# Later filter taps, eps as a bias, a last block by column halves and wider gathers in a Mamba block with a top-1 expert layer

## The chip, the cores and the metric

The kernel runs on one core of a Trainium2 chip. The metric is the device time of one execution in microseconds (us), as the median of several runs. The core's engines are written as in the profile: PE (TensorE, with its weight loads as PEld), DVE (VectorE), ACT (ScalarE), POOL (GpSimd) and SP (SyncE). They run side by side, each through its own queue in order, and wait for each other by semaphores.

## The reference

Two residual layers, each followed by a normalisation over 256 features, on 4096 tokens in one sequence:

```python
xz = input_tensor @ W_in                      # 256 -> 1024
conv_in, gated = xz[..., :512], xz[..., 512:]
convolved = silu(causal_conv(conv_in, 4 taps, per channel) + conv_b)
x_dbl = convolved @ W_x                       # 1 + 16 + 16 columns
delta = softplus(x_dbl[..., :1]);  Bm, Cm = x_dbl[..., 1:17], x_dbl[..., 17:]
deltaA  = exp(delta * A);  deltaBx = delta * Bm * convolved[..., :16]
h = deltaA * h + deltaBx;  y = sum(h * Cm)    # token after token
attn = ((y + convolved * D_param) * silu(gated)) @ W_out
x = layernorm(x + attn)
e = argmax(x @ Wr.T + br)                     # one of 8 experts
x = layernorm(x + relu(x @ W1[e].T + b1[e]) @ W2[e].T + b2[e])
```

The hidden width of an expert is 1024. layernorm is (x − mean) / sqrt(variance + 1e-05).

## The kernel before

**Two phases that overlap.** The tokens go through the Mamba block in 8 chunks of 512 (`TB`, `NB`). After that they are sorted by expert: 32 blocks of 128 rows (`SURE`), each of one expert, are gathered from the DRAM tensor `x1d`, put through the expert, and scattered to the output. The main loop runs over `k`, one chunk at a time, and works on several chunks at once: the in-projection of chunk k, the middle of chunk a = k−1, the end of chunk b = k−2, and the sorting of chunk c = k−3. The order of PE's instructions is that of the source (`manual_schedule` for PE); for the other engines a scheduler orders the instructions as it expects them to become ready, so an instruction's place in the source is only one of the things that set its place in a queue.

**One chunk.** `project(k, c)` makes 128 channels for c = 0 to 7. PE multiplies (`pm`, L722). For c < 4 they are the convolution's channels: ACT copies them to `xc` (L729) and makes the last tap with the bias into `acc` (L731), and DVE adds the other three taps (L735, three instructions over 128 by 512). Two projections later ACT makes their silu, `cv` (L742). For c of 4 and more ACT makes the silu of the gate, `sg` (L727). Between the projections stand the other chunks' steps:

- `gauge(a)` and `gauge_out(a)`: `x_dbl` of chunk a. PE multiplies and transposes (`px` L757, `pxo` L770), ACT copies, DVE adds two halves to `xd` (L780), and softplus follows as a chain of small instructions over 128 by 4: `e` (L785), its Exp on ACT (L786, for which ACT loads another table of functions), `s`, `w`, `q` on DVE (L792 to L801), and then `sr` (L804, L807), which holds delta, delta·B and C.
- `scan(a)`: PE transposes `sr` to `pt` (L816), ACT makes exp(delta·A), DVE runs the recurrence and multiplies with C to `hC` (L830).
- `gate(b)`: PE spreads `hC` as `py` (L842), DVE makes `cv` (L849), POOL and DVE the product `sg` (L854).
- `project_out(b, j)` for 128 tokens each: PE makes `po` (L890), DVE adds it to the input in `xb` (L894) and takes statistics (L898, L899). After the fourth, DVE adds eps (L904), ACT takes the root (L905), DVE makes `nma` (L908), ACT writes the normalised rows `x1` (L911), and SP stores them to `x1d`.
- `rank(c)`: the place of each token within its expert, as `row` (L971) and `col`; POOL makes the table `rowh` from `row` (L979), in four instructions, and for the last three chunks DVE does. `place(c)` (PE, L990) and a table with lookups turn them into the lists of row numbers, `tidx`, and of weights, `widx`.

**One expert block.** `prefetch` issues the indirect transfers on POOL: the block's rows `xg` (L500) and its expert's weights `we` (L517), two blocks ahead (`AHEAD`). `turn` transposes the rows (`pg`, L546), `hidden` multiplies with the first matrix (`ph`, L574) and ACT (L583, half 0) and DVE (L585, half 1) write relu into `hT`. `close` multiplies with the second matrix in 8 matmuls of 256 columns into `pe` (L599), DVE makes `xs`, the rows with the bias of the expert (L617). `finish` adds them to `r` (L624) and calls `layernorm` (L253 to L260): statistics and their aggregate on DVE, eps added on DVE (L257), root on ACT (L258), reciprocal and `y` on DVE. `scatter` writes `y` to its tokens by an indirect transfer on POOL (L637). At block 31, the last (`SURE - 1`), nothing is left to lie beside this chain.

**Longer blocks.** The blocks 17, 20, 23, 26 and 29 (`LONG`) take 32, 32, 32, 64 and 64 further rows (`ROOM`; `MORE` is its largest entry, 64), which a second gather brings (L500, named `long` in the profile) and a second layernorm and scatter finish. Tokens that find no room anywhere would go through blocks beyond the 32 under a condition.

**What the change touches.** `layernorm`, the list `further` in the lookup, `prefetch`, `close`, `scatter`, `project` with L735, L904 in `project_out`, and the main loop between `gauge_out(a)` and `project_out(b, 0)`.

Of the kernel before, what the change touches and what calls it, by code (L numbers as in the profile page):

```python
# [37 lines left out]
F32 = mybir.dt.float32  # L38
# [3 lines left out]
AF = mybir.ActivationFunctionType  # L42
ALU = mybir.AluOpType
# [4 lines left out]
P = 128  # L48
T, D = 4096, 256
DI, NS, KC = 512, 16, 4  # L50
NE, FF = 8, 1024
TB = 512
# [4 lines left out]
CC = DI // P  # L57
FC = FF // P
# [5 lines left out]
SURE = 32  # L64
# [10 lines left out]
ROOM = (32, 32, 32, 64, 64)  # L75
EXTRA, LESS, MORE = len(ROOM), min(ROOM), max(ROOM)
# [5 lines left out]
EPS = 1e-5  # L82
# [6 lines left out]
OC = OB + FC  # L89
# [10 lines left out]
def mamba_moe(  # L100
# [82 lines left out]
    def load_later():  # L183
# [6 lines left out]
        nc.sync.dma_start(brb, br.to_broadcast([P, NE]))  # L190
        nc.sync.dma_start(x1d[T : T + 1, :], lists[0:1, 0:D])

    ident = const.tile([P, P], F32, name="ident")
    make_identity(nc, ident)
    ones = const.tile([P, P], F32, name="ones")
# [50 lines left out]
        allow_small_or_imprecise_dtypes=True,  # L246
    )

    def layernorm(pool, rows, done, name):

        n = rows.shape[0]
        st = pool.tile([P, 6], F32, tag="st", name=f"st{name}")[0:n, :]
        nc.vector.bn_stats(st, rows)  # L253
        mv = pool.tile([P, 2], F32, tag="mv", name=f"mv{name}")[0:n, :]
        nc.vector.bn_aggr(mv, st)
        sd = pool.tile([P, 1], F32, tag="sd", name=f"sd{name}")[0:n, :]
        nc.vector.tensor_scalar(sd, mv[:, 1:2], EPS, None, ALU.add)  # L257
        nc.scalar.activation(sd, sd, AF.Sqrt)  # L258
        nc.vector.reciprocal(sd, sd)
        nc.vector.tensor_scalar(done, rows, mv[:, 0:1], sd, ALU.subtract, ALU.mult)  # L260

# [18 lines left out]
    def table(b0, nb, columns, rows, early):  # L280
# [155 lines left out]
        def lookup():  # L436

            pi = bank("tr", f"pi{b0}", 2)
            n = nb + longer
            for h in range(LH):  # L440
                nc.tensor.matmul(
                    pi[:, 0:n], lhsT=lists[:, h * P : (h + 1) * P], rhs=pick[:, h, :],
                    start=(h == 0), stop=(h == LH - 1),
                )
            codes = small("codes", [n])
            nc.scalar.copy(codes, pi[:, 0:n])
            half = small("half", [n])
            nc.vector.tensor_scalar(half, codes, 0.0, -float(T + 1), ALU.is_gt, ALU.mult)
            tidx = const.tile([P, n], I32, name=f"tidx{b0}")
            nc.vector.scalar_tensor_tensor(tidx, codes, float(T), half, ALU.add, ALU.add)  # L450
            for b in range(nb):
                index[b0 + b] = rows, tidx[:, order(b0, b)]
            for b, x in LONG.items() if longer else ():
                further[b] = tidx[0 : ROOM[x], nb + x : nb + x + 1]

        return lookup

# [35 lines left out]
    xgs, wes, turned, hid, last, open_, ys = {}, {}, {}, {}, {}, {}, {}  # L493


    xgf, openf, yf, ends_, wide_, xss, seldom_in = {}, {}, {}, {}, {}, {}, []
    current = 0

    def gather(to, rows, at):
        nc.gpsimd.indirect_dma_start(  # L500
            out=to, out_offset=None, in_=x1d[0:rows, :],
            in_offset=bass.IndirectOffsetOnAxis(ap=at, axis=0),
        )

    def prefetch(b):
        for n in range(b, min(b + AHEAD, SURE - 1) + 1):
            if n in index and n not in xgs:
                xgs[n] = m3.tile([P, D], F32, tag="xg", name=f"xg{n}", bufs=4)
                gather(xgs[n], *index[n])
                if n in LONG:  # L510
                    ends_[n] = a2.tile([P, CC, KC - 1 + TB], F32, tag="xc", name=f"long{n}")
                    ends_[n] = ends_[n].rearrange("p c t -> p (c t)")
                    xgf[n] = ends_[n][0 : more_of(n), 0:D]
                    gather(xgf[n], index[n][0], further[n])
            if n in weights and n not in wes:
                wes[n] = held_weights[n % SLOTS]
                nc.gpsimd.indirect_dma_start(  # L517
                    out=wes[n][:, :], out_offset=None, in_=experts,
                    in_offset=bass.IndirectOffsetOnAxis(ap=weights[n], axis=0),
                    bounds_check=NE * P - 1, oob_is_err=False,  # L520
                )

    def more_of(b):
        return ROOM[LONG[b]] if b in LONG else 0
# [64 lines left out]
    def close(b, half):  # L589
        we, hT = wes[b], hid[b]  # L590
        if half == 0:
            open_[b] = bank("o", f"pe{b}")
        py = open_[b]

        def out_weights(fc):
            return we[:, O2 + fc * D : O2 + (fc + 1) * D]

        for fc in range(half * FC // 2, (half + 1) * FC // 2):
            nc.tensor.matmul(  # L599
                py[:, 0:D], lhsT=hT[:, fc, 0:P], rhs=out_weights(fc),  # L600
                start=(fc == 0), stop=(fc == FC - 1),
            )
        if half == 0:
            return
        if b in LONG:

            openf[b], n = bank("o", f"pf{b}"), more_of(b)
            for fc in range(FC):
                g = fc * n % P
                nc.tensor.matmul(  # L610
                    openf[b][g : g + n, 0:D], lhsT=hT[:, fc, P:], rhs=out_weights(fc),
                    start=(fc < P // n), stop=(fc >= FC - P // n), tile_position=(0, g),
                )
        xss[b] = m2.tile([P, D], F32, tag="xs", name=f"xs{b}")

        with tc.issue_after(last[b].ins):
            nc.vector.tensor_tensor(xss[b], xgs[b], we[:, OC : OC + D], ALU.add)  # L617
        if b != SELDOM:
            finish(b)

# [12 lines left out]
            layernorm(m2, r, yf[b], f"f{b}")  # L633

    def scatter(b):
        for rows, at in ((ys[b], index[b][1]), *(((yf[b], further[b]),) if b in LONG else ())):
            moved = nc.gpsimd.indirect_dma_start(  # L637
                out=out, out_offset=bass.IndirectOffsetOnAxis(ap=at, axis=0),
                in_=rows, in_offset=None, bounds_check=T - 1, oob_is_err=False,
            )  # L640

            tc.declare_no_dep(moved.ins, group="rows", reason="blocks have no row in common")
            tc.add_to_no_dep_group("rows", moved.ins)
# [60 lines left out]

    def project(i, c):

        s = st[i]
        xTb = s["xTb"]  # L710
        if c == 0:
            if i == 0:
                s["xc"] = a2.tile([P, CC, KC - 1 + TB], F32, tag="xc", name="xc0")
                nc.gpsimd.memset(s["xc"][:, :, 0 : KC - 1], 0.0)
            s["cv"] = a3.tile([P, CC, TB], F32, tag="cv", name=f"cv{i}")
            s["sg"] = a3.tile([P, CC, TB], F32, tag="sg", name=f"sg{i}")
        xc, cv, sg = s["xc"], s["cv"], s["sg"]
        pm = bank("mm", f"pm{i}_{c}")

        for at in (slice(0, first), slice(first, TB)) if i == c == 0 else (slice(0, TB),):  # L720
            for dc in range(DC):
                nc.tensor.matmul(  # L722
                    pm[:, at], lhsT=win[:, dc, c * P : (c + 1) * P], rhs=xTb[:, dc, at],
                    start=(dc == 0), stop=(dc == DC - 1),
                )
        if c >= CC:
            evicted = nc.scalar.activation(sg[:, c - CC, :], pm, AF.Silu)  # L727
        else:
            nc.scalar.copy(xc[:, c, KC - 1 :], pm)  # L729
            acc = a3.tile([P, TB], F32, tag="acc", name=f"acc{i}_{c}")  # L730
            evicted = nc.scalar.activation(  # L731
                acc, pm, AF.Identity, scale=cw[:, c, KC - 1 : KC], bias=cb[:, c : c + 1]
            )
            for k in range(KC - 1):
                nc.vector.scalar_tensor_tensor(  # L735
                    acc, xc[:, c, k : k + TB], cw[:, c, k : k + 1], acc, ALU.mult, ALU.add
                )
            s["acc", c] = acc
        if ("acc", c - 2) in s:

            with tc.issue_after(evicted.ins):
                nc.scalar.activation(cv[:, c - 2, :], s["acc", c - 2], AF.Silu)  # L742
        if c == CC and i + 1 < NB:

            after = st[i + 1]["xc"] = a2.tile(
                [P, CC, KC - 1 + TB], F32, tag="xc", name=f"xc{i + 1}"
            )
            nc.gpsimd.tensor_copy(after[:, :, 0 : KC - 1], xc[:, :, TB : TB + KC - 1])
# [137 lines left out]
    def project_out(i, j):  # L886
# [14 lines left out]
            return  # L901
        mv = s_["mv"]
        sd = s_["sd"] = a2.tile([P, JT], F32, tag="sda", name=f"sda{i}")
        nc.vector.tensor_scalar(sd, mv[:, :, 1], EPS, None, ALU.add)  # L904
        nc.scalar.activation(sd, sd, AF.Sqrt)  # L905
        nc.vector.reciprocal(sd, sd)
        nm = a2.tile([P, JT], F32, tag="nma", name=f"nma{i}")
        nc.vector.scalar_tensor_tensor(nm, mv[:, :, 0], -1.0, sd, ALU.mult, ALU.mult)  # L908
# [103 lines left out]
    def have(i):  # L1012
        return 0 <= i < NB
# [4 lines left out]
    for k in range(NB):  # L1018
# [26 lines left out]
        project(k, 3)  # L1045
        if have(a):
            gauge_out(a)
        if have(b):
            project_out(b, 0)
        expert(fill[3])  # L1050
# [125 lines left out]
```

## Time and profile before

| what | value |
|---|---|
| median of 3 runs | 490.08 us (489.82 to 491.45) |
| the profiled execution | 486.77 us |
| its span | 485.0 us |
| mean granted PE clock | 0.996 |
| PE busy | 471.0 us (97%) |
| DVE busy | 346.9 us (72%) |
| ACT busy | 218.8 us (45%) |
| POOL busy | 186.9 us (39%) |
| DMA | 89.55 MB, mean 185 GB/s |

The span is that of the recorded instructions, in us from the first; the execution's own time is 1.8 us longer. In the views below, a group line gives the instructions' count, their busy time, the mean in ns, and the idle time of the engine before them with its releaser. A timeline line gives start, duration, engine, source line and operation, output and inputs with shapes, how many instructions are drawn together, and in brackets the idle time before with what ended it. A window's line gives the window and its length, then the busy time of PE, PEld, DVE, ACT and POOL with counts, the PE clock, the share of the DMA engines' time, and GB/s. A line of the view of waits gives the engine and instruction that waited, what it waited for, the total in us, the number of times and the longest.

### The profile page before, as it was taken

To read this page: it belongs to the slowest core of one execution; us is meant where nothing else is said; L and a number is where in the kernel's file an instruction comes from. 1 tells how busy PE (TensorE), PEld (TensorE's weight loads), DVE (VectorE), ACT (ScalarE), POOL (GpSimd) and SP (SyncE) were. 2 spreads that over 40 slices of the span, in tenths; PEclk is the share of its full clock that TensorE was granted. 3 is DMA by queue.
4 is the path that set the end of the run, shared out by engine and by line. 5 is a ranking of instruction groups with operands and counts; after the bars stand their busy time and mean duration, and the time that the engine had idled before them with its cause. 6 is when DMAs were issued, how large, how long until landed. Compare 5 with 4: busy or idle time off the path is not lost.

```text
span 485.0 us, 7589 instructions
## 1 busy us (share of the span) xinstructions
PE 471.0 (97%) x2602; PEld 351.9 (73%) x2602; DVE 346.9 (72%) x1160; ACT 218.8 (45%) x452; POOL 186.9 (39%) x193
## 2 busy tenths in 40 slices
PE   8999999999999999999999999999999999999993
PEld 5444555545454676776989999999989898989882
DVE  2577969797999997986989879554465656555362
ACT  3777678887778776655633122122121212112120
POOL 2001203444427454342524332444344456635531
PEclk9999999999999999999999999999999999999998
DMA  7401012030316926423577857999985289868800
GB/s 236 152 10 45 0 45 86 14 118 0 95 39 243 393 91 234 146 110 112 204 249 270 309 177 311 352 327 368 357 276 205 49 340 294 256 223 297 311 18 22
DMA packets 23049, 89.55 MB, mean 185 GB/s; under 512 B 4898, under 2 KB 14629, under 8 KB 19298
## 3 DMA queue, kind: packets, MB, share of 16 engines
q0 software_dynamic: 8672, 74.29, 42.4%
q1 hardware_dynamic: 13378, 14.50, 9.3%
q8 instruction: 21, 0.34, 0.3%
q10 hardware_dynamic: 960, 0.27, 0.3%
q14 instruction: 18, 0.15, 0.1%
HBM read 87.35 MB, written 9.54 MB: 200 GB/s over the span
## 4 chain that ended last, share of the span: by engine, by line
PE 73%; DVE 14%; issue 6%; DMA 3%; ACT 2%; POOL 1%; POOLq 0%; SPq 0%; ACTq 0%
PE ph L574 24%; PE pe L599 22%; PE pm L722 12%; PE po L890 8%; DVE acc L735 5%; DVE cv L849 2%; PE pg L546 2%; PE px L757 2%; DMA xg<-x1d,tidx 1%; DMA win<-in_W_in 1%; PE py L842 1%; PE pf L610 1%; PE pz L990 1%; DVE nma L908 1%; PE pt L816 1%
## 5 line engine op out<-in xcount | busy, mean ns | idle before, releaser
L722 PE MATMUL pm<-xTb,win 128*128 128x512 f32 (+1 forms) x260 | 121.3, 598 | 0.7 <-DMA win<-in_W_in 0.5
L574 PEld LDWEIGHTS ph<-xgT,we 128*128 128x128 f32 x864 | 100.7, 192 | 6.0 <-DVE stm L253 1.2
L574 PE MATMUL ph<-xgT,we 128*128 128x128 f32 x864 | 103.2, 276 | 0.0
L599 PE MATMUL pe<-we,hT 128*128 128x256 f32 x432 | 99.4, 381 | 0.0
L599 PEld LDWEIGHTS pe<-we,hT 128*128 128x128 f32 x432 | 79.7, 190 | 10.2 <-DVE lg L931 0.3
L735 DVE SCALAR_TENSOR_TENSOR acc<-xc,cw,acc 128x512 f32<-128x512 f32 x96 | 71.2, 771 | 16.5 <-ACT acc L731 16.1
L722 PEld LDWEIGHTS pm<-xTb,win 128*128 128x128 f32 x260 | 47.6, 192 | 47.5 <-issue 40.7
L517 POOL DMA_INDIRECT we<-in_experts,widx x32 | 33.9, 1058 | 89.2 <-DVE r L624 28.3
L258 ACT ACTIVATE sdm<-sdm 128x1 f32<-128x1 f32 x32 | 6.5, 202 | 131.0 <-DVE sdm L257 131.0
L890 PE MATMUL po<-wout,sg 128*128 128x264 f32 x256 | 64.1, 392 | 0.0
L854 POOL TENSOR_TENSOR sg<-cv,sg 128x512 f32<-128x512 f32 x22 | 33.9, 1544 | 59.2 <-DVE cv L849 44.1
L890 PEld LDWEIGHTS po<-wout,sg 128*128 128x128 f32 x256 | 46.0, 190 | 10.2 <-issue 2.9
L637 POOL DMA_INDIRECT out<-y,tidx x32 | 32.9, 1027 | 43.1 <-DVE y L260 26.8
L624 DVE TENSOR_TENSOR r<-pe,xs 128x256 f32<-128x256 f32 x32 | 13.5, 422 | 45.4 <-PE pe L599 45.2
L585 DVE TENSOR_SCALAR hT<-ph,we 128x128 f32<-128x128 f32 x108 | 31.5, 342 | 18.7 <-PE ph L574 18.4
L500 POOL DMA_INDIRECT xg<-x1d,tidx x32 | 32.0, 998 | 30.3 <-DVE tidx L450 5.7
L583 ACT ACTIVATE hT<-ph,we 128x128 f32<-128x128 f32 x108 | 31.0, 367 | 25.9 <-PE ph L574 23.3
L979 POOL TENSOR_SCALAR rowh<-lrow,row,code 128x256 f16<-128x256 bf16 x20 | 25.8, 1298 | 26.7 <-DVE row L971 26.7
L849 DVE SCALAR_TENSOR_TENSOR cv<-cv,dp,py 128x256 f32<-128x256 f32 x64 | 28.8, 469 | 2.4 <-PE py L842 2.4
L727 ACT ACTIVATE sg<-pm 128x512 f32<-128x512 f32 x32 | 19.1, 596 | 17.1 <-PE pm L722 14.8
L729 ACT COPY xc<-pm 128x512 f32<-128x512 f32 x32 | 18.6, 581 | 17.0 <-PE pm L722 16.9
L731 ACT ACTIVATE acc<-pm,cb,cw 128x512 f32<-128x512 f32 x32 | 25.1, 784 | 0.0
(221 smaller groups left out, 616.5 us busy)
## 6 DMA issues: line engine op xcount, KB each, us to landing
xb<-in_x SPq DMA_DIRECT2D x8, 512.0 KB, 4.8
x1d<-x SPq DMA_DIRECT2D x8, 512.0 KB, 4.8
xTb<-in_xT SPq DMA_DIRECT2D x7, 512.0 KB, 3.7
win<-in_W_in SPq DMA_DIRECT2D x1, 512.0 KB, 6.2
we<-in_W_outT SPq DMA_DIRECT2D x1, 512.0 KB, 4.8
wout<-in_W_out SPq DMA_DIRECT2D x1, 512.0 KB, 5.7
we<-in_experts,widx POOLq DMA_INDIRECT x32, 10.2
xg<-x1d,tidx POOLq DMA_INDIRECT x32, 6.2
```

The lines of the kernel that those rows point to most:

```text
L500: nc.gpsimd.indirect_dma_start(out=to, out_offset=None, in_=x1d[0:rows, :], in_offset=bass.IndirectOffsetOnAxis(ap=at, axis=0),)
L517: nc.gpsimd.indirect_dma_start(out=wes[n][:, :], out_offset=None, in_=experts, in_offset=bass.IndirectOffsetOnAxis(ap=weights[n], axis=0), ...
L574: nc.tensor.matmul(ph[:, n * w : (n + 1) * w], lhsT=we[:, at : at + P], rhs=xgT[:, dc * w : (dc + 1) * w], start=(dc == 0), stop=(dc == DC ...
L583: nc.scalar.activation(hT[:, fc, :], ph[:, n * w : (n + 1) * w], AF.Relu, bias=bias)
L585: last[b] = nc.vector.tensor_scalar(hT[:, fc, :], ph[:, n * w : (n + 1) * w], bias, 0.0, ALU.add, ALU.max)
L599: nc.tensor.matmul(py[:, 0:D], lhsT=hT[:, fc, 0:P], rhs=out_weights(fc), start=(fc == 0), stop=(fc == FC - 1),)
L637: moved = nc.gpsimd.indirect_dma_start(out=out, out_offset=bass.IndirectOffsetOnAxis(ap=at, axis=0), in_=rows, in_offset=None, bounds_chec ...
L722: nc.tensor.matmul(pm[:, at], lhsT=win[:, dc, c * P : (c + 1) * P], rhs=xTb[:, dc, at], start=(dc == 0), stop=(dc == DC - 1),)
L735: nc.vector.scalar_tensor_tensor(acc, xc[:, c, k : k + TB], cw[:, c, k : k + 1], acc, ALU.mult, ALU.add)
L849: nc.vector.scalar_tensor_tensor(cv[:, c, at], cv[:, c, at], dp[:, c : c + 1], py[:, 0 : TB // 2], ALU.mult, ALU.add,)
L854: eng.tensor_tensor(sg[:, c, :], cv[:, c, :], sg[:, c, :], ALU.mult)
L890: nc.tensor.matmul(po[:, 0 : D + NE], lhsT=sg[:, c, j * P : (j + 1) * P], rhs=wout[:, c, :], start=(c == 0), stop=(c == CC - 1),)
```

## The change

Four edits are made.

1. `eps` is a tile of 128 by 1, filled once on POOL. In `layernorm` and in `project_out` the addition of eps on DVE is gone (L257, L904), and ACT's root reads the variance itself with `eps` as its bias.
2. `project(k, 3)` no longer issues its three taps. A new function `taps` does, and for the fourth group of channels the main loop calls it after `gauge_out(a)`.
3. The last block's second product is made by column halves. `close` is called twice for a block, as before; for block 31 each call now does all 8 matmuls on 128 columns, where it did 4 on 256. The first call makes `xs`, and each adds its half to `r` and takes that half's statistics; the second runs the rest of layernorm over both.
4. The gather of further rows always takes 64 rows (`MORE`). The transposes, products and the scatter use as many as before (`more_of`).

```diff
+    eps = const.tile([P, 1], F32, name="eps")
+    nc.gpsimd.memset(eps, EPS)
...
-    def layernorm(pool, rows, done, name):
+    def layernorm(pool, rows, done, name, st=None):
         n = rows.shape[0]
-        st = pool.tile([P, 6], F32, tag="st", name=f"st{name}")[0:n, :]
-        nc.vector.bn_stats(st, rows)
+        if st is None:
+            st = pool.tile([P, 6], F32, tag="st", name=f"st{name}")[0:n, :]
+            nc.vector.bn_stats(st, rows)
         mv = pool.tile([P, 2], F32, tag="mv", name=f"mv{name}")[0:n, :]
         nc.vector.bn_aggr(mv, st)
         sd = pool.tile([P, 1], F32, tag="sd", name=f"sd{name}")[0:n, :]
-        nc.vector.tensor_scalar(sd, mv[:, 1:2], EPS, None, ALU.add)
-        nc.scalar.activation(sd, sd, AF.Sqrt)
+        nc.scalar.activation(sd, mv[:, 1:2], AF.Sqrt, bias=eps[0:n, :])
...
-                further[b] = tidx[0 : ROOM[x], nb + x : nb + x + 1]
+                further[b] = tidx[0:MORE, nb + x : nb + x + 1]
...
+                    gather(ends_[n][0:MORE, 0:D], index[n][0], further[n])
                     xgf[n] = ends_[n][0 : more_of(n), 0:D]
-                    gather(xgf[n], index[n][0], further[n])
...
+        def add_rows():
+            xss[b] = m2.tile([P, D], F32, tag="xs", name=f"xs{b}")
+            with tc.issue_after(last[b].ins):
+                nc.vector.tensor_tensor(xss[b], xgs[b], we[:, OC : OC + D], ALU.add)
+        if b == SURE - 1:
+            at = slice(half * D // 2, (half + 1) * D // 2)
+            for fc in range(FC):
+                nc.tensor.matmul(
+                    py[:, at], lhsT=hT[:, fc, :], rhs=out_weights(fc)[:, at],
+                    start=(fc == 0), stop=(fc == FC - 1),
+                )
+            if half == 0:
+                add_rows()
+                halves.append(m2.tile([P, D], F32, tag="r", name=f"r{b}"))
+                halves.append(a2.tile([P, 2, 6], F32, tag="sta", name=f"st{b}"))
+            r, sts = halves
+            nc.vector.tensor_tensor(r[:, at], py[:, at], xss[b][:, at], ALU.add)
+            nc.vector.bn_stats(sts[:, half, :], r[:, at])
+            if half == 1:
+                ys[b] = m2.tile([P, D], F32, tag="y", name=f"y{b}")
+                layernorm(m2, r, ys[b], f"m{b}", sts)
+            return
...
-        xss[b] = m2.tile([P, D], F32, tag="xs", name=f"xs{b}")
-        with tc.issue_after(last[b].ins):
-            nc.vector.tensor_tensor(xss[b], xgs[b], we[:, OC : OC + D], ALU.add)
+        add_rows()
...
-        for rows, at in ((ys[b], index[b][1]), *(((yf[b], further[b]),) if b in LONG else ())):
+        for rows, at in ((ys[b], index[b][1]), *(((yf[b], further[b][0 : more_of(b), :]),) if b in LONG else ())):
...
+    def taps(i, c):
+        acc, xc = st[i]["acc", c], st[i]["xc"]
+        for k in range(KC - 1):
+            nc.vector.scalar_tensor_tensor(
+                acc, xc[:, c, k : k + TB], cw[:, c, k : k + 1], acc, ALU.mult, ALU.add
+            )
...
-            for k in range(KC - 1):
-                nc.vector.scalar_tensor_tensor(
-                    acc, xc[:, c, k : k + TB], cw[:, c, k : k + 1], acc, ALU.mult, ALU.add
-                )
             s["acc", c] = acc
+            if c < CC - 1:
+                taps(i, c)
...
-        nc.vector.tensor_scalar(sd, mv[:, :, 1], EPS, None, ALU.add)
-        nc.scalar.activation(sd, sd, AF.Sqrt)
+        nc.scalar.activation(sd, mv[:, :, 1], AF.Sqrt, bias=eps)
...
         project(k, 3)
         if have(a):
             gauge_out(a)
+
+        taps(k, CC - 1)
         if have(b):
             project_out(b, 0)
```

More of the change, by code (lines that the diff above doesn't have):

```diff
@@ L493, in mamba_moe @@
     xgs, wes, turned, hid, last, open_, ys = {}, {}, {}, {}, {}, {}, {}
-    xgf, openf, yf, ends_, wide_, xss, seldom_in = {}, {}, {}, {}, {}, {}, []
+    xgf, openf, yf, ends_, wide_, xss, seldom_in, halves = {}, {}, {}, {}, {}, {}, [], []
     current = 0
```

## The prediction

> **What bounds the kernel.** First the table of windows: busy time of each engine by stretch, PE first.
>
> ```profile
> 100.00:140.00 40.00, 39.26 (x156) 21.02 (x156) 37.02 (x101) 31.93 (x54) 14.61 (x12) 1.00 0.21 66
> 140.00:180.00 40.00, 39.27 (x185) 23.68 (x184) 37.24 (x134) 30.48 (x52) 24.02 (x19) 1.00 0.57 221
> ...
> 260.00:420.00 160.00, 160.00 (x1108) 146.49 (x1107) 102.78 (x396) 31.15 (x112) 74.24 (x74) 1.00 0.78 280
> ...
> 475.00:485.00 10.00, 2.13 (x10) 1.52 (x8) 1.93 (x7) 0.20 (x1) 0.99 (x1) 0.79 0.04 13
> ```
>
> TensorE (second figure) is full everywhere but in the chunk loop, which lacks 0.7 us in 40, and in the last 8 us. VectorE comes nearest to it between 100 and 180, 37 of 40. An edit can pay only by removing PE waits or by shortening the tail. The view of waits by engine gives what there is:
>
> ```profile
> PE pt L816 <- DVE mva L899: 1.4, 2, 0.7
> ...
> PE pg L546 <- DMA xg<-x1d,tidx: 0.5, 1, 0.5
> ```
>
> `pt` reads `sr`, not `mva`: the timeline of VectorE and PE in chunk step k=4 shows L807, which writes `sr`, end at 118.48, and `pt` go at 118.62.
>
> ```profile
> 118.14 0.34 DVE L807 TENSOR_TENSOR sr<-xd,sr 128x64 f32<-128x64 f32 x1
> 118.40 0.17 DVE L899 BATCH_NORM_AGGREGATE mva<-sta 128x2 f32<-128x6 f32 x1
> 118.62 0.61 PE L816 MATMUL pt<-ident,sr 128*80 128x128 f32 x4 [0.69 <-DVE mva L899]
> ```
>
> The same stall is 0.67 at 91.14 (k=3), and 0.16 at 145.59 (k=5, put to `here`): 0.67 + 0.69 + 0.16 = **1.52 us**, all that the taps can win at `pt`. The stalls `py` on hC and `sg` on L854 are not on their path.
>
> **The taps.** Three taps (L735, 771 ns each by their group, about 2.0 us together) go behind the head of `gauge_out`. Nothing is added: `xd` (L780) and `e` stand three taps earlier on VectorE, and taps fill the time in which ScalarE loads the table (1.28) and does Exp (0.21). The built order still has all three ahead of L807, but puts one `xb` addition and one `bn_stats` (start to start 0.34 each) behind it, and covers gaps in the chain s…q, whose steps stand 0.26 apart where 0.08 is the cost of one: L807 comes 0.7 to 1.2 us earlier, which covers each stall of up to 0.69. ScalarE takes Exp ahead of a silu `sg` and a `cv`; the PSUM bank they free is needed over 3 us later: nothing.
>
> Of what is moved: `row` (L971) now stands behind five more small chain operations, 0.35 to 0.6 us later against PE. POOL waits for it with `rowh` and, right behind, with the first weights:
>
> ```profile
> 142.62 5.24 POOL L979 TENSOR_SCALAR rowh<-lrow,row,code 128x256 f16<-128x256 bf16 x4 [7.14 <-DVE row L971]
> 148.05 1.27 POOL L517 DMA_INDIRECT we<-in_experts,widx  x1 [0.18 <-issue]
> ...
> 166.09 1.47 POOL L500 DMA_INDIRECT xg<-x1d,tidx  x1 [5.68 <-DVE tidx L450]
> ```
>
> The DMA queues are nearly full from 150 to 171, and the first rows, issued at 166.09, land 7.27 us later behind those weights; PE waits for them at 173.50 for 0.54, the wait at `pg` above. So the stalls at 91 and 118 won (1.36) bring the weights forward by only 1.36 − 0.6 = 0.76 to 1.36 − 0.35 = 1.01, and the rest is waited for at `pg`: I take **−0.9**, since that wait is a row of this trace, and keep −1.52 as the other end. SP's x1d stores move with their chunk. In the expert phase rows and weights come over 4 us early: nothing.
>
> VectorE also has `s` (L792), which waits for Exp, ahead of `row` now; behind it queue `row`, L807 and everything else. VectorE reaches `s` 2.7 us (k=2) to 3.9 us (k=4, 5) after `xd`; `e` came 2.05 to 2.65 us after it. Slack 0.65 to 1.25: nothing, while it lasts. In the drain ScalarE's root for a block stands behind four x1 activations and a table load; the hidden rows it delays are ready 0.1 us ahead of their use: nothing, on thin cover.
>
> **Eps as bias.** It takes away L257 and L904. Under a full PE that is nothing (in the loop `cv` waits 0.27 for PE's `py` behind it). In the tail the step L257 to root is 0.19. Against it stands the dearer root: the activation with pointers for scale and bias (L731) takes 784 ns where the copy of the same shape (L729) takes 581, so 0.10 for each pointer. Tail: −0.09. The new memset of one column on POOL lies under the first loads (PE starts at 6.6 us).
>
> **The last block by halves.** The timeline of the tail, before:
>
> ```profile
> 473.51 3.62 PE L599 MATMUL pe<-we,hT 128*128 128x256 f32 x16
> ...
> 477.17 0.42 DVE L624 TENSOR_TENSOR r<-pe,xs 128x256 f32<-128x256 f32 x1 [2.00 <-PE pe L599]
> 477.62 0.43 DVE L253 BATCH_NORM_STATS2 stm<-r 128x6 f32<-128x256 f32 x1
> ...
> 478.30 0.15 DVE L257 TENSOR_SCALAR sdm<-mvm 128x1 f32<-128x1 f32 x1
> 478.49 0.20 ACT L258 ACTIVATE sdm<-sdm 128x1 f32<-128x1 f32 x1 [5.38 <-DVE sdm L257]
> ...
> 481.16 0.99 POOL L637 DMA_INDIRECT out<-y,tidx  x1 [7.60 <-issue]
> ```
>
> 16 records at 0.216 become 32 of 128 columns at 0.112 (L574's pace in full stretches): 3.57 for 3.46, half 0 done at 475.46. Both halves lie in one bank, and in the built program the first matmul of half 1 waits on VectorE for `r` of half 0. That runs 475.50 to 475.79 (0.42 less 128 columns, 0.13); PE resumes at 475.85 and `r` of half 1 starts at about 477.86, not 477.17: **+0.69**. Behind it r and bn_stats are half as long (−0.13 each); the eps edit gives −0.09. Tail: 0.69 − 0.26 − 0.09 = **+0.34**.
>
> Here the Trainium skill speaks against the change. "PSUM — Partial Sum Buffer", section "PSUM bank collisions raise a hardware error", wants PSUM guarded by bank and quadrant, not by address: a VectorE read of the left columns may not run beside a matmul writing the right ones. By that rule, which the built wait obeys, the tail is +0.34. By the rows alone, `r` of half 0 under PE's second half, PE would end at 477.24 and `r` start 0.11 late: 0.11 − 0.26 − 0.09 = −0.24. I take the rule, because the wait is built in; no run here shows such a read side by side.
>
> After `y` (478.93 to 479.34) the trace has 1.8 us before the last scatter, which it puts to issue; other scatters start 0.28 after their `y`. If something else than `y` fixes that time, the tail's +0.34 vanishes in it, or the gap shrinks. From the trace neither is excluded: 0 to −1.5, taken as 0.
>
> **64 rows.** Three gathers (blocks 17, 20, 23) go from 32 to 64 rows. POOL takes 867 to 1057 ns for all five, 32 and 64 rows alike; 3 × 32 KB is 0.1 MB, 0.3 us at the 280 GB/s of that stretch, used two blocks (14 us) after issue, landed after a median of 6.9: nothing. Cover gone, it would be at most that 0.3.
>
> **Sum.** −0.9 + 0.34 = −0.56 at the middle; with pt's whole gain −1.18, with none of it +0.34. The chain is the profiled run's, 486.77 us about a span of 485.0; the median of the runs shown is 490.08, 3.3 above, and the same difference is put to it. I take −0.7, between the two sums and nearer to the first: 489.4.
>
> **Rivals.**
> - *All of it arrives.* `xg` is limited by its own issue (7.27 against a median of 6.2 for such gathers) and moves along with `tidx`; the tail's cost falls into the 1.8 us before the last scatter. Then −1.52 and some of that gap, up to −3.0; middle −2.2: 487.9. Against it: the queues are full until 171.
> - *Nothing arrives*: the weights take back all, or L807 isn't the one that comes last: 490.1 to 490.4. For it: L807 gains only by what the scheduler swaps.
> - *VectorE's queue stops at `s`* (the slow side). Place: k=3 to 5, VectorE at 37 of 40. If ScalarE does a silu and a `cv` (0.60 + 0.63) and a table load (1.28) before Exp, `e` is 2.5 late, against slack of 0.65 to 1.25: 1.3 to 1.9 us in which row, L807 and `xb` stand, less about 1.0 that L807 had won: 0.6 in each of three steps, 0.6 more at `pg`, and the tail: 1.8 + 0.6 + 0.34 = +2.7, 492.8. It decides as soon as `e` is over about 1.2 us late. Against it: the built order has Exp first.
>
> **Chances and range.** About 0.3% (1.5 us) is what a measurement can tell from no change: 488.6 to 491.5. Forecast 0.42 (489.4; own range 488.4 to 490.4, 0.08 of it under 488.6), all arrives 0.28, nothing 0.04, queue stops 0.26. Faster 0.08 + 0.28 = 0.36; same 0.34 + 0.04 = 0.38; slower 0.26. The range 487.2 to 491.9 leaves out the far ends of both outer cases.
>
> **What would show it.** `pt` without stalls at about 91, 118, 145; the wait at `pg` grown to about 1.1; L807 ahead of an `xb`; a PE gap of 0.4 in the last block, `r` of half 1 0.69 later against the block's first `pe`; roots of 0.29. An idle VectorE ahead of L792 would show the slow rival; a last scatter right behind `y` the fast one. A stall that moved to `py` or `po` would make the sum wrong.

## The result and the profile after

The changed kernel takes 487.0 us (median of 9 runs, 486.12 to 489.64), the kernel before in the same runs 490.8 us (488.65 to 492.03). The ratio is **0.9937** (95% interval 0.9914 to 0.996): faster by 0.6%, about 3 us. A second set of runs beside the kernel before, below, gave 0.9903 (0.9882 to 0.9924).

The profiled execution of the changed kernel has a span of 484.4 us where that of the kernel before had 485.0. That is less than the medians say, and shows how little one profile decides: the profile of the kernel before came from an execution of 486.8 us, faster than every timed one. So the view of the waits comes first here, and the totals after it. Of the changed kernel it has these lines among its first (engine, instruction, what it waited for, total in us, times, longest):

```profile
PE pe L628 <- ACT hT L586: 1.0, 1, 1.0
...
PE pg L549 <- DMA xg<-x1d,tidx: 0.6, 1, 0.6
...
PE prx L894 <- DVE rk L994: 0.4, 1, 0.4
PE pe L612 <- DVE r L621: 0.4, 1, 0.4
```

The `pt` stalls behind VectorE are gone. `pg` waits 0.6 where it was 0.5. New are `prx`, the stop between the halves (L612, which the prediction had at 0.4), and a wait of 1.0 for `hT` in the expert phase. The timeline of chunk step k=4 shows what became of the largest `pt` stall:

```profile
115.75 0.23 DVE L838 TENSOR_TENSOR sr<-xd,sr 128x64 f32<-128x64 f32 x1
115.89 0.43 DVE L925 TENSOR_TENSOR xb<-po,xb 128x264 f32<-128x264 f32 x1
...
116.30 0.38 PE L907 MATMUL pf<-ident,rx 128*128 128x128 f32 x2
116.52 0.60 PE L847 MATMUL pt<-ident,sr 128*80 128x128 f32 x4
```

L838 is the former L807. It now comes ahead of the last `xb` addition and ends 0.54 us before `pt` starts, with no idle time of PE between `pf` and `pt`; before, it ended 0.14 us ahead of `pt`, and PE had been idle for 0.69. The line of `pf` in the kernel before gives the shift:

```profile
117.55 0.38 PE L876 MATMUL pf<-ident,rx 128*128 128x128 f32 x2
```

L807 ended 0.93 after the start of that `pf` (118.48), L838 ends 0.32 ahead of its own (115.98): 1.25 us sooner against PE.

The end of the program, in the same view, first the lines of `y` and of the scatters of blocks 30 and 31 in the kernel before that the prediction does not show:

```profile
471.90 0.41 DVE L260 TENSOR_SCALAR y<-r,mvm,sdm 128x256 f32<-128x256 f32 x1
...
472.59 0.97 POOL L637 DMA_INDIRECT out<-y,tidx  x1 [5.59 <-DVE y L260]
...
478.93 0.41 DVE L260 TENSOR_SCALAR y<-r,mvm,sdm 128x256 f32<-128x256 f32 x1
```

and the changed kernel:

```profile
472.29 0.41 DVE L262 TENSOR_SCALAR y<-r,mvm,sdm 128x256 f32<-128x256 f32 x1
...
474.00 1.95 PE L612 MATMUL pe<-we,hT 128*128 128x128 f32 x16
...
474.52 0.99 POOL L663 DMA_INDIRECT out<-y,tidx  x1 [6.13 <-issue]
...
475.98 0.29 DVE L621 TENSOR_TENSOR r<-pe,xs 128x128 f32<-128x128 f32 x1 [0.33 <-PE pe L612]
...
476.33 2.05 PE L612 MATMUL pe<-we,hT 128*128 128x128 f32 x16 [0.38 <-DVE r L621]
478.42 0.29 DVE L621 TENSOR_TENSOR r<-pe,xs 128x128 f32<-128x128 f32 x1 [1.81 <-PE pe L612]
...
479.32 0.29 ACT L260 ACTIVATE sdm<-mvm,eps 128x1 f32<-128x1 f32 x1 [5.71 <-DVE mvm L258]
...
479.85 0.41 DVE L262 TENSOR_SCALAR y<-r,mvm,sdm 128x256 f32<-128x256 f32 x1
480.53 0.97 POOL L663 DMA_INDIRECT out<-y,tidx  x1 [5.03 <-DVE y L262]
```

PE stops for 0.38 between the halves; from the block's first `pe` to the end of `y` it takes 480.26 − 474.00 = 6.26 us, where it was 479.34 − 473.51 = 5.83. But the last scatter now follows `y` after 0.27 instead of 1.82 us, and the scatter of block 30, which ends nothing, has come to stand 1.82 behind its own `y` (472.70 to 474.52), where it was 0.28. The 1.8 us have not gone: they **moved one scatter forward**, off the end. Which edit did that is the first question for the experiments.

What the stop waits for can be narrowed down in the kernel before, where it lies alone. This is the window from 479.4 to 481.1:

```profile
479.40:481.10 1.70, 0.00 (x0) 0.00 (x0) 0.00 (x0) 0.00 (x0) 0.00 (x0) 0.90 0.00 0
```

No engine runs an instruction in it and no DMA queue moves a packet, those that fetch instructions included (the last packet of any queue before the scatter is at 474.65). So, as far as the trace records these, POOL waits neither for a transfer still under way, nor for code being fetched, nor for another engine.

The profiled pair then sums up as follows. At the first `ph` PE is 2.1 us ahead (0.5 of it from the first transfers at the start of the program), at 303 us 2.5; between there and 467 us it loses 3.0, so that block 31 starts 0.49 late; the tail costs 0.43 and the end gives 1.55 back: 0.49 + 0.43 − 1.55 = −0.63, the difference of the spans.

### The profile page after: what moved, and what is told of

It reads as the page before. It is cut to its first block, busy times and chain, and to the rows that moved or that the text cites. A ratio compares the mean times of both kernels' runs of the same rounds, so it can differ in the third digit from the quotient of the medians.

```text
span 484.4 us, 7580 instructions
## 1 busy us (share of the span) xinstructions
PE 471.3 (97%) x2618; PEld 352.9 (73%) x2618; DVE 340.3 (70%) x1117; ACT 224.0 (46%) x453; POOL 185.9 (38%) x194
## 5 line engine op out<-in xcount | busy, mean ns | idle before, releaser
L628 PE MATMUL pe<-we,hT 128*128 128x256 f32 x416 | 96.1, 381 | 1.4 <-ACT hT L586 1.0
L628 PEld LDWEIGHTS pe<-we,hT 128*128 128x128 f32 x416 | 76.7, 190 | 11.9 <-ACT hT L586 1.2
L736 DVE SCALAR_TENSOR_TENSOR acc<-xc,cw,acc 128x512 f32<-128x512 f32 x96 | 72.9, 780 | 16.0 <-ACT acc L764 15.6
L260 ACT ACTIVATE sdm<-mvm,eps 128x1 f32<-128x1 f32 x32 | 9.5, 296 | 143.7 <-DVE mvm L258 118.7
L885 POOL TENSOR_TENSOR sg<-cv,sg 128x512 f32<-128x512 f32 x22 | 32.8, 1495 | 59.3 <-DVE cv L880 45.9
```

The source lines that it names most:

```text
L628: nc.tensor.matmul(py[:, 0:D], lhsT=hT[:, fc, 0:P], rhs=out_weights(fc), start=(fc == 0), stop=(fc == FC - 1),)
L736: nc.vector.scalar_tensor_tensor(acc, xc[:, c, k : k + TB], cw[:, c, k : k + 1], acc, ALU.mult, ALU.add)
L885: eng.tensor_tensor(sg[:, c, :], cv[:, c, :], sg[:, c, :], ALU.mult)
```

## Experiments

Ratios are to the kernel before in the same runs, with 95% intervals.

**The taps alone.**

```diff
             s["acc", c] = acc
+            if c < CC - 1:
+                taps(i, c)
...
             gauge_out(a)
+
+        taps(k, CC - 1)
```

> The kernel before with the later taps alone. Theory A (the taps carry the gain of the chunk loop): the stalls of pt at about 91, 118 and 145 are gone, PE is about 1.5 to 2.1 us ahead at the first ph (175.72 before), and the ratio is about 0.996, two thirds of the whole change's 0.9937. Rival B (fewer VectorE instructions, the eps edit, carry it): at most one of the stalls goes, PE is under 0.7 us ahead at 175, and the ratio is 0.999 to 1. Rival C (the gain lies in the end of the program): PE is ahead as in A, but the ratio is over 0.998.

Ratio 0.9958 (0.994 to 0.9976). The stalls are gone, here at k=4:

```profile
118.08 0.38 PE L881 MATMUL pf<-ident,rx 128*128 128x128 f32 x2
118.30 0.60 PE L821 MATMUL pt<-ident,sr 128*80 128x128 f32 x4
```

Measured step by step against the kernel before, PE gains 0.65 at `pt` of k=3, 0.85 at k=4, loses 0.45 at `prx`, gains 0.32 at `pt` of k=5 and 0.28 up to the first `ph`: **1.65 us**, or 1.37 without the last, since the wide gathers alone, which leave the loop as it was, show 0.21 at the same place. The lead that was expected at the first `ph` is not in the trace all the same: PE stands at 176.18 there, 0.46 behind, because its start came 1.17 later and a wait of 0.95 for `sg` lies between. Neither is counted to the taps. Waits of 0.5 to 1.8 for `sg` come and go in these traces, in that of the halves alone too, where nothing of the chunk loop is changed, and one of the two traces of the changed kernel has it and the other not. Theory A holds so far as the stalls and the ratio go, with the 0.45 as its only loss. Where that comes from, the timeline of VectorE, ScalarE and PE in step 5 shows, first in the kernel before, then in the second trace of the changed kernel:

```profile
140.64 0.18 DVE L964 TENSOR_TENSOR rk<-pr,oh 128x32 f32<-128x32 f32 x1
...
142.00 0.15 DVE L792 TENSOR_SCALAR s<-e 128x4 f32<-128x4 f32 x1
```

```profile
138.25 0.21 ACT L817 ACTIVATE e<-e 128x4 f32<-128x4 f32 x1
...
138.89 0.73 DVE L736 SCALAR_TENSOR_TENSOR acc<-xc,cw,acc 128x512 f32<-128x512 f32 x1
...
139.55 0.16 DVE L823 TENSOR_SCALAR s<-e 128x4 f32<-128x4 f32 x1
139.62 0.17 DVE L930 BATCH_NORM_AGGREGATE mva<-sta 128x2 f32<-128x6 f32 x1
139.71 0.16 DVE L994 TENSOR_TENSOR rk<-pr,oh 128x32 f32<-128x32 f32 x1
...
139.92 0.64 PE L894 MATMUL prx<-xTb,wr 128*32 128x256 f32 x8 [0.42 <-DVE rk L994]
```

`rk` reads the PSUM tile `pr`, and `prx` waits for `rk`: `pr` and `prx` take turns in the two banks that the program gives to the tag `tr`. Ahead of `rk` on VectorE now stand the last tap (0.73), `s` and `mva`. `pr` had been done since 135.91 and `e` for over a microsecond, so it is not the Exp that holds `rk` up but the mere place in the queue, and the tap most of all. Before, `rk` came 1.4 us ahead of `s`, and `prx` started with no idle PE.

In step k=3 of the changed kernel the Exp came close to stopping VectorE all the same, here in its first trace:

```profile
83.16 0.59 ACT L760 ACTIVATE sg<-pm 128x512 f32<-128x512 f32 x1
...
83.65 0.62 ACT L773 ACTIVATE cv<-acc 128x512 f32<-128x512 f32 x1
...
85.58 0.21 ACT L817 ACTIVATE e<-e 128x4 f32<-128x4 f32 x1
...
85.82 0.17 DVE L823 TENSOR_SCALAR s<-e 128x4 f32<-128x4 f32 x1
```

ScalarE takes a silu `sg` and a `cv` ahead of the Exp and its table load, as the slow rival had it. `e` is ready at 85.79, 3.10 us after `xd` started (82.69), and `s` starts 0.03 later: no slack is left, but VectorE shows no idle time ahead of `s` either. In steps 4 and 5 ScalarE takes `sg` alone ahead of the Exp, and `s` starts 1.08 us after `e`.

**Eps as a bias alone.**

```diff
-        nc.vector.tensor_scalar(sd, mv[:, 1:2], EPS, None, ALU.add)
-        nc.scalar.activation(sd, sd, AF.Sqrt)
+        nc.scalar.activation(sd, mv[:, 1:2], AF.Sqrt, bias=eps[0:n, :])
```

(and the same in `project_out`).

> The kernel before with eps as a bias alone. Theory A: the three stalls of pt stay as they are (0.6 to 0.7 at 91 and 118), nothing at 175 (within 0.4 us), roots 0.29 instead of 0.20, ratio 0.999 to 1.001. Rival B: the stalls shrink by more than half and PE is 0.7 to 2 us ahead at 175, ratio 0.996 to 0.998.

Ratio 0.9981 (0.9966 to 0.9997), between the two theories. The root takes 0.29 us. One stall shrank, that of k=3, from 0.67 to 0.18:

```profile
89.43 0.38 PE L877 MATMUL pf<-ident,rx 128*128 128x128 f32 x2
89.99 0.61 PE L817 MATMUL pt<-ident,sr 128*80 128x128 f32 x4 [0.18 <-DVE sr L808]
```

In VectorE's timeline `xd` of that step comes behind a row of six taps where in the kernel before it came behind seven, and L808 ahead of the last `bn_stats`. The edit took a few instructions away, and the scheduler put others on VectorE in another order. That 0.5 and the 0.09 of the tail make 0.6 of the 0.9 us that the ratio stands for, within its interval. In the whole change the taps remove that stall anyway.

**The column halves alone.** The edit is that of `close`, with the addition of eps kept.

> The kernel before with the column halves of the last block alone. Theory A: PE stops for about 0.4 between the halves; from the first pe of block 31 to the end of y it takes 6.3 instead of 5.83 us, and the last scatter comes later by up to that 0.45 or, if the 1.8 us before it are cut to 0.3 as in the changed kernel's trace, earlier by up to 1. Ratio 1.000 to 1.001 in the first case. Rival C (the end carries the gain): the gap before the last scatter is 0.3 and the ratio 0.996 to 0.998.

Ratio 1.0001 (0.9978 to 1.0024). From the first `pe` to the end of `y` it takes 484.10 − 477.74 = 6.36 us, PE's stop is 0.38, and the scatter still comes 1.82 after `y`:

```profile
483.69 0.41 DVE L261 TENSOR_SCALAR y<-r,mvm,sdm 128x256 f32<-128x256 f32 x1
485.92 0.98 POOL L661 DMA_INDIRECT out<-y,tidx  x1 [8.12 <-issue]
```

The halves cost half a microsecond and do not move the stop of the scatter; their price in the time is below what these runs tell.

**The halves in two PSUM banks**, all else as in the changed kernel.

```diff
             at = slice(half * D // 2, (half + 1) * D // 2)
+            if half == 1:
+                py = bank("o", f"pe{b}_1")
             for fc in range(FC):
```

> The changed kernel with the two column halves of the last block in two PSUM banks. If the shared bank alone makes PE wait between the halves, the wait of 0.38 and the refilling behind it go, r of the first half lies under the second half's matmuls, and from the first pe of block 31 to the end of y it takes 5.6 to 5.75 us instead of 6.26; ratio 0.001 lower than the changed kernel's, 0.9925 to 0.993. If PE waits for something else there (the hidden rows hT, the sum xs), the gap stays and the ratio is 0.9937.

```profile
475.35 3.74 PE L614 MATMUL pe<-we,hT 128*128 128x128 f32 x32
...
477.34 0.29 DVE L623 TENSOR_TENSOR r<-pe,xs 128x128 f32<-128x128 f32 x1 [0.33 <-PE pe L614]
...
479.12 0.29 DVE L623 TENSOR_TENSOR r<-pe,xs 128x128 f32<-128x128 f32 x1 [1.17 <-PE pe L614]
...
480.55 0.41 DVE L262 TENSOR_SCALAR y<-r,mvm,sdm 128x256 f32<-128x256 f32 x1
```

PE's 32 records run without a stop, `r` of the left half (477.34 to 477.63) lies under them, and the stretch takes 480.96 − 475.35 = **5.61 us**. So the shared bank alone made the stop, which with what hangs on it cost 6.26 − 5.61 = 0.65 us. The interval of the ratio, 0.9898 (0.9858 to 0.9937), is too wide to show that difference in the time.

**The gathers of 64 rows alone, and the changed kernel without them.**

```diff
-                further[b] = tidx[0 : ROOM[x], nb + x : nb + x + 1]
+                further[b] = tidx[0:MORE, nb + x : nb + x + 1]
...
+                    gather(ends_[n][0:MORE, 0:D], index[n][0], further[n])
```

> The kernel before with the gathers of 64 rows alone. In the traces so far the last scatter comes 1.8 us after its y in the kernel before and in the three with one of the other edits; in the changed kernel and the one with two banks, the only two with the wider gathers, it comes 0.3 after, and the scatter one block earlier has the 1.8. Theory D (the wider gathers shift by 96 rows a point in POOL's stream of row transfers at which it stops for 1.5 us more): here too the last scatter comes 0.3 after y and the last but one 1.8, PE's times up to block 31 are as before, and the ratio is about 0.997. Rival E (the place of the stop comes from the number of instructions, or from all edits together): 1.8 stays at the last scatter, ratio 0.999 to 1.001.

> The changed kernel with the gathers of 32 rows for the blocks that need 32. Theory D: the stop of 1.8 us is back before the last scatter, and the time is 1.5 us more than the changed kernel's: ratio 0.9968 where that has 0.9937. Rival E: the last scatter still comes 0.3 after y, ratio 0.9937.

With the wide gathers alone the ratio is **0.9959** (0.9937 to 0.998); the changed kernel without them has 0.9962 (0.9946 to 0.9978) where the changed kernel in the same runs has 0.9903. The timeline of VectorE and POOL at the end shows `y` and its scatter for blocks 30 and 31, first with the wide gathers alone:

```profile
473.17 0.41 DVE L260 TENSOR_SCALAR y<-r,mvm,sdm 128x256 f32<-128x256 f32 x1
475.39 0.99 POOL L638 DMA_INDIRECT out<-y,tidx  x1 [7.12 <-DVE hT L586]
480.19 0.41 DVE L260 TENSOR_SCALAR y<-r,mvm,sdm 128x256 f32<-128x256 f32 x1
480.88 0.97 POOL L638 DMA_INDIRECT out<-y,tidx  x1 [4.51 <-DVE y L260]
```

and for block 31 in the changed kernel without them:

```profile
477.71 0.41 DVE L262 TENSOR_SCALAR y<-r,mvm,sdm 128x256 f32<-128x256 f32 x1
479.95 0.98 POOL L662 DMA_INDIRECT out<-y,tidx  x1 [8.12 <-issue]
```

Theory D holds against E: the edit that was priced at nothing moves the stop from the last scatter to the one before, alone and among the other edits, and is worth 1.55 us in the traces.

**128 rows in all five gathers**, to see whether the stop's place goes by rows.

```diff
-                further[b] = tidx[0:MORE, nb + x : nb + x + 1]
+                further[b] = tidx[:, nb + x : nb + x + 1]
...
-                    gather(ends_[n][0:MORE, 0:D], index[n][0], further[n])
+                    gather(ends_[n][:, 0:D], index[n][0], further[n])
```

> The changed kernel with 128 rows in each of the five gathers of further rows (320 rows and more beyond the changed kernel's). Theory D (POOL stops after a certain number of transferred rows): so many rows more move the stop past the last three scatters (y of block 31, y of 30, the further rows of 29), so neither y of 31 nor y of 30 has it (0.3 each), and an earlier one has; the time is that of the changed kernel, ratio 0.990 to 0.994. Rival F (what matters is that all gathers have one size): the stop stays at y of block 30, 1.8 us.

Ratio 0.9914 (0.9878 to 0.9949). The stop is now at `y` of block 29 (its end at 462.31, POOL free at 462.19, the scatter at 464.09), and the scatters of 30 and 31 follow at 0.28:

```profile
461.22 0.97 POOL L663 DMA_INDIRECT out<-seldom,tidx  x1 [0.30 <-issue]
...
461.73 0.58 DVE L262 TENSOR_SCALAR y<-r,mvm,sdm 128x256 f32<-128x256 f32 x1
...
464.09 0.98 POOL L663 DMA_INDIRECT out<-y,tidx  x1 [1.90 <-issue]
...
466.49 0.91 POOL L663 DMA_INDIRECT out<-long,tidx  x1 [1.42 <-DVE long L262]
...
472.00 0.97 POOL L663 DMA_INDIRECT out<-y,tidx  x1 [4.60 <-DVE y L262]
...
479.56 0.97 POOL L663 DMA_INDIRECT out<-y,tidx  x1 [6.58 <-DVE y L262]
```

| gathers of further rows | traces | stop of 1.8 us before the scatter of |
|---|---|---|
| 32, 32, 32, 64, 64 | 6 of 6 (two of the kernel before, the taps, eps and halves alone, and the changed kernel without the wide gathers) | block 31 |
| 64 in all | 6 of 6 (two of the changed kernel, the wide gathers alone, two with two banks, one with rank ahead) | block 30 |
| 128 in all | 1 of 1 | block 29 |

More rows move the stop to an earlier scatter; rival F, one size for all, falls. Its length hardly changes: from `y` (or the end of POOL's last instruction, where that is later) to the scatter it is 1.78 to 1.82 us in all 13 traces. The exact rule stays open: rows were the only thing varied, and bytes and descriptors vary with them; counting 128 rows for each scatter and 64 for the further rows, no single number of rows fits all three places, unless some rows (those whose number lies outside the output, for instance) don't count.

**Both kernels once more.**

> The changed kernel itself, for a second profile and beside the others on one chip: ratio 0.992 to 0.996; 0.3 us before the last scatter; no stall at pt of chunks 3 to 5; and, if the stop of VectorE at the second addition of further rows in block 29 (3.6 us in its first trace) belongs to the program and not to that execution, the same stop again, with pe of block 30 waiting about 1 us for hT.

> The kernel before itself, for a second profile. Its first one took 486.8 us where the median is 490.8. If the stop of VectorE in block 29 belongs to every program here, it shows in this trace, about 3.4 us long, and the span is near 489; if it came with the edits, it doesn't.

The changed kernel again: 483.7 us (4 runs), ratio 0.9903 (0.9882 to 0.9924), 0.28 before the last scatter, no stall at `pt` of these steps, `pg` 0.9. The kernel before again: span 485.9, `pt` 1.4 and `pg` 0.7 as in its first trace, and the stop before its last scatter. Neither has the stop of VectorE in block 29 that the first trace of the changed kernel shows:

```profile
460.70 0.41 DVE L262 TENSOR_SCALAR y<-r,mvm,sdm 128x256 f32<-128x256 f32 x1
...
464.69 0.88 DVE L658 TENSOR_TENSOR long<-pf,long 64x256 f32<-64x256 f32 x2 [3.58 <-remote]
...
466.27 0.30 ACT L260 ACTIVATE sdf<-mvf,eps 64x1 f32<-64x1 f32 x1 [5.80 <-DVE mvf L258]
```

`pf` was done at 460.9, and no row of the trace releases L658 at 464.69. ScalarE's `sdf` waits for it, and `hT` of block 30 stands behind `sdf` on ScalarE, which is PE's 1.0 at `pe`. The same stop, 3.3 to 3.6 us, stands in the traces of the taps, eps and halves alone and of the three of kernels with two banks, that of the next experiment included; in those of the taps and the halves alone ScalarE stops as well, for 4.2 and 4.3. Between 303 and 473 us PE loses 2.2 to 3.0 us in each of these seven traces, not all of it at that stop; in the six others it loses nothing, but for 1.1 in the one with 128 rows. The stop is missing in the second trace of the changed kernel, which is the same program, so the edits alone don't decide it. Both traces of the kernel before lack it too. What makes it was not found, nor whether the change makes it rarer or more frequent.

**Rank ahead of the head of gauge_out**, in the kernel with two banks, beside that kernel once more.

```diff
         project(k, 3)
+        if have(c):
+            rank(c)
         if have(a):
             gauge_out(a)
...
-        if have(c):
-            rank(c)
```

> The changed kernel with the last block's halves in two PSUM banks, again, for the comparison with the next one on one chip. From the first pe of block 31 to the end of y 5.6 us as in its first trace (6.26 with one bank), ratio 0.989 to 0.991.

> The same, with the call of rank(c) moved ahead of gauge_out(a). In the changed kernel VectorE's s, which waits for Exp, stands ahead of rk, and PE's prx waits 0.42 us for rk in chunk step 5; row comes later too, and with it the first weights and the rows that pg waits for (0.9 us). If that queueing is what the taps give back, prx's 0.42 goes, POOL's rowh of that step starts 1 us or more sooner against PE, and pg's wait shrinks: 0.4 to 1 us in all, ratio 0.001 to 0.002 under the last. If the wait at pg is set by the rows' own transfer, only 0.4 goes. If something of rank now stops gauge_out instead, a stall at pt comes back (0.3 to 0.7 in each of three steps), and the ratio is above the last.

Two banks: 0.993 (0.9905 to 0.9956), 480.98 − 475.38 = 5.60 from `pe` to `y`. With rank ahead: 0.9948 (0.9925 to 0.9971), no gain. The 0.4 at `prx` is gone and POOL's `rowh` starts at 137.94 where it was 142.34, 4.4 us sooner; `pg` no longer waits for its rows. But in the next step `pxo` waits for ScalarE to empty a bank of `tr`:

```profile
159.90 0.66 PE L803 MATMUL pxo<-ident,pxs 128*128 128x128 f32 x4 [1.01 <-ACT codes L448]
```

and `pt` waits 0.4 and 0.3 again. The 1.0 at `pxo` alone is more than the 0.4 that went at `prx`.

## Why the prediction came out as it did

The predicted time was 489.4 us, with faster, same and slower at 0.36, 0.38 and 0.26. The change is faster by 0.6%: 487.0 us lies 0.2 below the low end of the range, and what the interval of the ratio covers (485.9 to 488.1, on 490.08) reaches into it. The likeliest case was too slow by 2.4 us and its own range, from 488.4, missed; that the whole range reaches so near the result is owed to a rival's low side. By its steps:

- **Stalls at `pt`: right.** All three went, 1.5 us, by the mechanism stated: L807 ahead of an `xb` addition and a `bn_stats`, 1.25 us sooner at k=4 where 0.7 to 1.2 were forecast.
- **The give-back at `pg`: wrong in size and place.** 0.5 to 0.75 was taken off because `row`, and so the first weights, would fall behind. `pg` waited for its rows 0.3 to 1.0 us in the traces with the taps, where it did, and 0.3 to 0.8 in those without: no difference that they show. `row` did move behind small chain operations, but in step 5, where the first weights hang on it, PE fell behind together with it: 0.42 at `prx`. POOL's `rowh` of that step came 1.77 us sooner in the changed kernel's first trace, as far ahead as PE. The wait that was new was `rk` behind three instructions on VectorE, and with it a PSUM bank that PE needed, which no step had. The taps' −0.9 was −1.4 to −1.65.
- **The slow rival: its place was right, its force wasn't.** The prediction had ScalarE take the Exp first; in fact a `sg` goes ahead of it in steps 4 and 5, and a `sg` and a `cv` in step 3, where the slack of 0.65 to 1.25 was down to 0.03. VectorE still did not stop for `e` in these steps, `rk` stood behind `s` but was held up by a tap, and the price was 0.4 once. In step 3 the forecast's "nothing" held by luck.
- **Eps: right in the tail** (root 0.29; 0.1 for the pointer, as the rows L731 and L729 had it). Its "nothing" under a full PE missed that a shorter VectorE queue is also a differently ordered one: alone it took 0.5 from one stall.
- **Halves: right.** Stop 0.38 for 0.4, `r` of the second half 478.42 − 474.00 = 4.42 after the first `pe` where it was 3.66: +0.76 for +0.69; tail +0.43 for +0.34. To go by the rule on PSUM banks of the Trainium skill ("PSUM — Partial Sum Buffer", section "PSUM bank collisions raise a hardware error") was right for the program as built: with one bank the wait is there, and with two it goes and the tail falls to 5.61, 0.22 below the 5.83 of before, where the prediction by the rows alone had −0.24. What a read beside a matmul in one bank would do, no run here shows.
- **The 1.8 us before the last scatter, taken as 0, and the 64 rows, priced at nothing: the step that failed.** The range's low side allowed for the gap with 0 to −1.5; measured were −1.55. The wide gathers were costed by POOL's time, bytes and landing, all of which are indeed nothing; that they also shift where POOL's stream of row transfers stops was not asked, though the gap stood in the trace as a wait that nothing explained. The rival "all of it arrives" came nearest, with 487.9, in part by luck: it had the tail's cost fall into the gap, and the runs show the gap moved off the end.

With the measured terms the prediction's sum would read −1.4 to −1.65 for the taps, +0.43 for the tail and −1.55 for the gap: −2.5 to −2.8, inside the −2.0 to −4.2 that the interval of the ratio makes on 490.08.

By parts, the ratios measured alone multiply to 0.9958 × 0.9981 × 1.0001 × 0.9959 = 0.9899, against 0.9937 and 0.9903 measured for the whole, whose intervals meet from 0.9914 to 0.9924. The taps and the gathers alone make 0.9958 × 0.9959 = 0.9917 of it.

## What to carry to other kernels

An idle stretch at the very end that no row of the trace explains is worth an experiment before it is put down as fixed: here it was a stop of POOL whose place depends on how many rows were moved before it, and 96 unused rows put it where it costs nothing. When an instruction moves ahead of others on an engine, ask which PSUM bank the overtaken ones free; here, with two banks under one tag, a reader of 0.16 us that came late stopped PE for 0.42. And the halves of this accumulation overlapped with their reader only when they lay in different banks.

## What the runs showed of the hardware

- Near the end of the program POOL starts one scatter 1.78 to 1.82 us after its data is ready where others take 0.28. It is the same scatter in both traces of a program wherever there are two, and an earlier one when earlier gathers carry more rows (table above). In the kernel before no engine and no DMA queue is active in that time.
- VectorE stops for 3.3 to 3.6 us in block 29 in 7 of 13 traces, ahead of an instruction whose inputs are ready; the same program has it in one execution and not in another. PE loses 3.0 us over the expert phase in the first trace of the changed kernel and 2.3 in that of the taps alone, and none in the second of the changed kernel. The timed runs of either kernel spread by some 3.5 us; that this stop makes the spread was not shown.
- Two traces, the second of the kernel before and that of the wide gathers alone, have a granted PE clock of 0.57 and 0.66 between 44 and 48 us, and PE loses about 1.6 us there in each; the others have 1.00.
